# Attention scores in 64x32 tiles: 32 matmuls and one masked copy a pass, where 16 matmuls and three copies stood

## The chip, the core and the metric

The kernel runs on one core of a Trainium2 chip. A core has engines that work side by side, each through its own queue of instructions: PE (TensorE, matmuls, and PEld, its weight loads), DVE (VectorE), ACT (ScalarE), POOL (GpSimd) and SP, which here only issues DMAs. Matmul results land in PSUM; DVE and ACT bring them to SBUF. The metric is the device time of one execution in microseconds, as the median of the runs; less is better.

## What is computed

One layer in fp32 on x of shape (4, 2048, 256): a gated linear attention with a decaying state, a residual and a layer norm, then a feed-forward part with three coupling cycles, another residual and layer norm. The change touches the attention alone. Cut to that:

```python
Q = (xn @ WQ.T + bQ).reshape(batch, seq_len, N_HEADS, D_HEAD)   # 16 heads of 64
K = (xn @ WK.T + bK).reshape(batch, seq_len, N_HEADS, D_HEAD)
V = (xn @ WV.T + bV).reshape(batch, seq_len, N_HEADS, D_HEAD)
gate = silu(xn @ Wg.T + bg)
alpha = sigmoid(alpha_logit)
def step(h, qkv):
    q, k, v = qkv
    h = alpha[None, :, :, None] * h + k[:, :, :, None] * v[:, :, None, :]
    o = jnp.einsum('bhi,bhij->bhj', q, h)
    return (h, o)
...
y = (o * gate).reshape(batch, seq_len, D_INNER) @ WO.T + bO
```

The kernel does not step through the tokens. It cuts them into chunks of 64. Within a chunk, the output of a query at place t is the sum over keys at places s <= t of a decayed score times the value; what came before the chunk enters through the state. The decay between a key and a query is a product of a factor on the key and one on the query, each kept near 1 by measuring it from the middle of a block of 32 tokens.

## The kernel before

**Tiling.** A group is 512 tokens (G), eight chunks of 64 (C), each of two blocks of 32 (H). There are 4 x 4 groups, and in each the heads go in eight pairs (HP): 128 passes of the main loop in `fast_program` (L1060), which runs when the decay rates are mild (a flag computed at the start; a second program, for other rates, is not run here). A pass has 128 partitions: two heads of 64.

**What a pass does.** `inter` (L955, matmuls at L963) applies the state to the queries, in 64*64 tiles, into the PSUM tile `pu`. `all_scores` (L552) makes the scores of the pass in the PSUM tile `sc` through `pairs` (L541, matmuls at L547). `keys` (L600) transposes the next pass's keys with four matmuls (L604); `copy_first` (L557) and `copy_own` (L565) bring the scores to the SBUF tile `A`; `decayed` (L607, the multiplication is at L609) makes the next pass's decayed keys `KE` on DVE between the two. `values` (L192) projects a part of the values. `between` (L914) puts in steps of the output projection (L653) and the feed-forward part (L754 to L877) by an allowance of time kept in the code. `products` (L973, matmuls at L980) multiplies scores and values on top of `pu`; `updates` (L614, L620) makes the next pass's state updates in `sc`; `gated` (L985) takes `pu` out; `new_states` (L996, L630) steps the states; `projections` (L464, matmuls at L454) makes keys, queries and gate for the pass after next, on PE, with ACT taking them out (L468, L472, L484) and POOL scaling the queries (L500, L510, L514).

**Order.** The engines PE, DVE, ACT and POOL run in the order in which this code calls them (`manual_schedule`); waits between engines are put in by semaphores. `sc` has one buffer, shared by the scores and the updates; `A` has two, used in turn, filled with zeros once at the start.

**The scores.** For each of the four pairs of chunks (i) there are four matmuls, one for each head h and each chunk c of the pair. The stationary operand is the 64 features by 64 keys of the chunk; the moving one is 64 features by 96 columns, the tile `QF`: the chunk's 64 queries, each scaled from the middle of its own block, and then its 32 second-half queries once more, scaled for the keys of the first block (written at L510 and L514). The result is 64 keys by 96 columns: columns 0 to 63 are right for keys and queries of one block, columns 64 to 95 for first-block keys by second-block queries. The rest is not used.

**The copies.** `copy_first` takes columns 64 to 95 of the first block's keys to columns 32 to 63 of `A`, with one ACT copy for each chunk of a pair (32 partitions each, L563). `copy_own` then copies columns 0 to 63 over `A` on DVE where a mask says so (L568). The mask `masks["in"]` (L422 to L427) is 1 where the query is not before the key and both lie in one block, and elsewhere `A` keeps what it has: ACT's copy, or zero.

Of the kernel before, what the change touches and what calls it, by code (L numbers as in the profile page):

```python
# [37 lines left out]
F32 = mybir.dt.float32  # L41
# [3 lines left out]
ALU = mybir.AluOpType  # L45
AX = mybir.AxisListType

P = 128
# [6 lines left out]
C = 64  # L55
H = C // 2
# [3 lines left out]
NT = G // P  # L60
HT = 2 * NT
# [12 lines left out]
def post_norm_layer(ctx: ExitStack, tc: tile.TileContext, a: dict, out: bass.AP):  # L74
    nc = tc.nc
    x = a["x"]
# [148 lines left out]
    with ExitStack() as first:  # L225
        work = first.enter_context(tc.tile_pool(name="first", bufs=1))
# [87 lines left out]
    def layer(fast, inside):  # L314
        pool = inside.enter_context(tc.tile_pool(name="fixed", bufs=1))
        work = inside.enter_context(tc.tile_pool(name="work", bufs=1))
# [3 lines left out]
        def fixed(name, shape, dtype=F32):  # L320
            return pool.tile(shape, dtype, tag=name, name=name)
# [7 lines left out]
        def two_banks(tag, bufs):  # L329
            return psum.tile([P, 2, 512], F32, tag=tag, name=tag, bufs=bufs)  # L330
# [9 lines left out]
        def load_x(b, g):  # L340
            X[b, g] = tokens_at(b, g)
            nc.sync.dma_start(out=X[b, g], in_=tokens(b, g))

        def norm_x(b, g):

            xn[b, g] = xns[(b * NG + g) % 2]
            for _ in norm_steps(work, pj, X[b, g], xn[b, g], 4):
                yield
            residual(X[b, g])
            yield  # L350
# [27 lines left out]
        masks, qtab, ktab = {}, {}, {}  # L378
        blocks = {}

        def block_of(w):
            if w not in blocks:
                tw = work.tile([P, C], F32, tag="cs", name="tw", bufs=2)
                sw = fixed(f"sw{w}", [P, 1])
                for o, v in ((tw, trow), (sw, scol)):
                    if w > 1:
                        sh = work.tile(list(v.shape), I32, tag="t", name="sh", bufs=3 if fast else 2)
                        nc.vector.tensor_scalar(sh, v, w.bit_length() - 1, None, ALU.logical_shift_right)
                        v = sh
                    nc.vector.tensor_copy(o, v)  # L390
                blocks[w] = tw, sw
            return blocks[w]

        def mask(key, w, back, r, lo):

            tw, sw = block_of(w)
            masks[key] = fixed(f"mask{key[0]}_{key[1]}", [P, C // r * (r - lo)], U8)
            nc.vector.tensor_scalar(
                masks[key].rearrange("p (n x) -> p n x", x=r - lo),
                tw.rearrange("p (n l) -> p n l", l=r)[:, :, lo:], float(back), sw,  # L400
                ALU.subtract, ALU.is_equal,
            )

        def repeated(name, v, n):

            w = v.shape[2]
            if n == 1:
                return v
            t = fixed(name, [P, HP, n * w])
            nc.vector.tensor_copy(  # L410
                t.rearrange("p h (n w) -> p h n w", w=w), v.unsqueeze(2).to_broadcast([P, HP, n, w])
            )
            return t
# [6 lines left out]
        if fast:  # L420

            t1, s1 = block_of(1)  # L422
            th, sh = block_of(H)
            after = work.tile([P, C], F32, tag="t", name="after", bufs=3)
            nc.vector.tensor_scalar(after, t1, s1, None, ALU.is_ge)
            masks["in"] = fixed("mask_in", [P, C], U8)
            nc.vector.scalar_tensor_tensor(masks["in"], th, sh, after, ALU.is_equal, ALU.mult)  # L427
        else:
            mask((0, 0), 1, 0, C, 0)
            mask((1, 0), 1, 1, 2, 1)  # L430
            for w, r in STAGES[:2]:
                for o in range(r - 1):
                    mask((w, o), w, o + 1, w * r, (o + 1) * w)
            for w, r in STAGES:
                ktab[w] = repeated(f"ktab{w}", down[:, :, C - w : C], r - 1)
                for o in range(r - 1):
                    qtab[w, o] = repeated(
                        f"qtab{w}_{o}", up[:, :, w * o : w * o + w], (r - 1 - o) * C // (w * r)
                    )
# [22 lines left out]
        KF, QF = {}, {}  # L462
# [78 lines left out]
        def pairs(ps, k, q, col):  # L541

            n = q.shape[2]
            for i in range(NT):
                for h, c in ((0, 0), (1, 1), (0, 1), (1, 0)):
                    r = slice(h * 64, (h + 1) * 64)
                    tc.keep_in_program_order(nc.tensor.matmul(  # L547
                        ps[c * 64 : (c + 1) * 64, h, i * P + col : i * P + col + n],
                        k[r, 2 * i + c, :], q[r, 2 * i + c, :], start=True, stop=True,
                    ))  # L550

        def all_scores(it):  # L552
            ps = two_banks("sc", 1)
            pairs(ps, KF.pop(it), QF.pop(it), 0)
            return ps

        def copy_first(ps, A):  # L557

            pv = ps.rearrange("p h (i x) -> p (h i) x", x=P)
            av = A.rearrange("p h i t -> p (h i) t")  # L560
            for c in range(2):
                r = slice(c * C, c * C + H)
                nc.scalar.copy(av[r, :, H:], pv[r, :, C : C + H])  # L563

        def copy_own(ps, A):  # L565
            pv = ps.rearrange("p h (i x) -> p (h i) x", x=P)
            av = A.rearrange("p h i t -> p (h i) t")
            nc.vector.copy_predicated(av, masks["in"].unsqueeze(1).to_broadcast([P, HT, C]), pv[:, :, 0:C])  # L568

        def scores(it, n, A):  # L570

# [35 lines left out]
        def decayed(pt, it):  # L607
            ke = work.tile([P, NT, P], F32, tag="KE", name="KE", bufs=1)
            nc.vector.tensor_mul(  # L609
                ke, pt.rearrange("p (i x) -> p i x", i=NT), at(dtok, it[2], [P, NT, P])  # L610
            )
            return ke
# [290 lines left out]
        def add(queue, steps):  # L903
            queue.append([steps, next(steps)])
# [103 lines left out]
        def follow(n, k):  # L1008
            return its[n + k] if n + k < len(its) else None
# [50 lines left out]
        def fast_program():  # L1060


            groups = [(b, g) for b in range(B) for g in range(NG)]
            norms = {}

            def norm(k):
                if k < len(groups):
                    norms.setdefault(k, norm_x(*groups[k]))
                    next(norms[k])

            load_x(*groups[2])
            projections(its[0])
            KE[its[0]] = decayed(keys(its[0]), its[0])
            projections(its[1])
            ahead = new_states(its[0], updates(KE.pop(its[0]), its[0]))
            for n, it in enumerate(its):
                b, g, hp = it
                k = n // HP
                nxt, then = follow(n, 1), follow(n, 2)
                A = As[n % 2]  # L1080
                po = inter(it, *ahead)
                sc = all_scores(it)
                if nxt:
                    pt = keys(nxt)
                copy_first(sc, A)
                if nxt:
                    KE[nxt] = decayed(pt, nxt)
                copy_own(sc, A)
                if hp < 4:
                    values(b, g, 1, hp)  # L1090
                elif k + 1 < len(groups):
                    values(*groups[k + 1], 0, hp - 4)
                if hp == 7:
                    norm(k + 2)
                between(("pe", "dve", "act"), 1.4)
                products(it, po, A)
                if nxt:
                    us = updates(KE.pop(nxt), nxt)
                gated(it, po)
                if hp % 4 == 3:  # L1100
                    add(posts, post(b, g, hp // 4))
                if nxt:
                    ahead = new_states(nxt, us)
                if then:
                    projections(then)
                vector = 2.8
                if k == 0 and hp < 4:
                    vector = 0.0
                    if hp == 0:
                        residual(X0)  # L1110
                        ffn_constants()
                    norm(1)
                if hp == 4 and k and k + 2 < len(groups):
                    load_x(*groups[k + 2])
                if hp > 4:
                    norm(k + 2)
                    vector = 1.4
                between(("pe", "dve"), vector)

            while posts or nets or couples:  # L1120
                for queue, m in ((posts, 0), (nets, 0), (couples, 0), (couples, 1)):
                    if len(queue) > m and queue[m][1][2]():
                        run(queue, m)
# [45 lines left out]
```

## Time and profile before

| what | value |
|---|---|
| median of 3 runs | 1962.02 us (1960.25 to 1963.20) |
| profiled execution | 1961.66 us |
| its span in the profile | 1959.9 us |
| mean granted PE clock | 0.981 |
| instructions | 48150, of them 21070 matmuls and as many weight loads |
| DMA | 20 GB/s over the span |

The span runs from the first instruction to the last that the profiler saw; the rest of the execution lies around it. A group's row names line, engine, operation, what is written and read, the tile of the array for matmuls (rows*columns), shapes and count; after the bar come the busy time in us and the mean of one instruction in ns, after the next bar the engine's idle time before these instructions and what ended it. Ends of matmuls are modelled, so that one record is longer than the time until the next begins: a row's busy time is the union of its records. Some other groups of a pass, in the same form:

```profile
L500 POOL TENSOR_TENSOR qd<-QA,up 128x512 f32<-128x512 f32 x128 | 160.5, 1254 | 1169.9 <-ACT QA L472 1151.0
L468 ACT ACTIVATE KT<-pj,bK 128x512 f32<-128x512 f32 x128 | 87.9, 687 | 481.8 <-PE pj L454 481.8
L609 DVE TENSOR_TENSOR KE<-pj,dtok 128x512 f32<-128x512 f32 x128 | 88.1, 688 | 234.7 <-PE pj L604 234.4
L980 PE MATMUL pu<-A,V 64*64 64x64 f32 x4096 | 90.5, 227 | 39.2 <-DVE A L568 39.2
```

The chain that ended last is followed back from the last instruction to what released it, or to the one before it on its engine; it tells which work set the end.

### The profile page before, as it was taken

What the parts mean: (1) busy time and instruction counts of PE and PEld (TensorE: products, weight loads), DVE (VectorE), ACT (ScalarE), POOL (GpSimd) and SP (SyncE); (2) the same over time, 40 slices, a digit from 0 to 9 for tenths busy, and PEclk for the clock granted to TensorE, in tenths of its full rate; (3) what the DMA queues carried; (4) which work ended last, traced back from release to release, by engine and by line L of the source; (5) the groups of instructions that cost most, each with busy time, mean ns of one, the idle gap of its engine ahead of it and who ended that gap; (6) DMA issues with size and microseconds to landing.
All of it is one profiled execution on the core that took longest, in us unless ns stands there. A gap on an engine that the chain in (4) does not pass through costs nothing.

```text
span 1959.9 us, 48150 instructions
## 1 busy us (share of the span) xinstructions
PE 1860.1 (95%) x21070; PEld 1074.5 (55%) x21070; DVE 1216.3 (62%) x3054; ACT 812.4 (41%) x1299; POOL 452.7 (23%) x436
## 2 busy tenths in 40 slices
PE   7999999998999999999999999999999999999975
PEld 3565655655555555555555555555555555555531
DVE  4665656665775567755576656764558755666455
ACT  3223242222454445444345445544345544444344
POOL 1222222222222222222222222222212222122100
PEclk9999999999999999999999999999999999999986
DMA  4000000000011000100001000000000100000002
GB/s 155 2 2 23 2 23 2 23 2 23 2 34 33 2 23 2 45 23 2 23 2 45 23 2 23 21 30 17 12 13 12 39 18 12 2 23 34 1 11 67
DMA packets 27419, 41.67 MB, mean 21 GB/s; under 512 B 4032, under 2 KB 22336, under 8 KB 27200
## 3 DMA queue, kind: packets, MB, share of 16 engines
q1 hardware_dynamic: 26192, 38.48, 5.8%
q8 instruction: 168, 2.75, 0.6%
q14 instruction: 51, 0.42, 0.1%
q10 hardware_dynamic: 1008, 0.02, 0.0%
HBM read 21.72 MB, written 16.78 MB: 20 GB/s over the span
## 4 chain that ended last, share of the span: by engine, by line
PE 83%; DVE 11%; ACT 2%; issue 2%; POOL 1%; DMA 0%; DVEq 0%; ACTq 0%; POOLq 0%; SPq 0%
PE pj L454 31%; PE pj L653 11%; PE pj L192 9%; PE pj L754 6%; PE pu L963 4%; PE pu L980 4%; PE pj L798 4%; PE sc L547 4%; PE pj L604 3%; PE sc L620 3%; PE pj L804 1%; DVE t L781 1%; DVE u L785 1%; PE pj L813 1%; DVE states L630 1%
## 5 line engine op out<-in xcount | busy, mean ns | idle before, releaser
L500 POOL TENSOR_TENSOR qd<-QA,up 128x512 f32<-128x512 f32 x128 | 160.5, 1254 | 1169.9 <-ACT QA L472 1151.0
L468 ACT ACTIVATE KT<-pj,bK 128x512 f32<-128x512 f32 x128 | 87.9, 687 | 481.8 <-PE pj L454 481.8
L454 PE MATMUL pj<-xn,wK 128*128 128x512 f32 x512 | 258.1, 627 | 1.7 <-DVE sw L390 1.7
L454 PE MATMUL pj<-xn,wQ 128*128 128x512 f32 x512 | 240.6, 592 | 0.0
L454 PE MATMUL pj<-xn,wg 128*128 128x512 f32 x512 | 240.6, 592 | 0.0
L192 PE MATMUL pj<-wV,xn 128*128 128x512 f32 x496 | 235.2, 597 | 0.0
L609 DVE TENSOR_TENSOR KE<-pj,dtok 128x512 f32<-128x512 f32 x128 | 88.1, 688 | 234.7 <-PE pj L604 234.4
L630 DVE SCALAR_TENSOR_TENSOR states<-states,up,sc 128x64 f32<-128x64 f32 x768 | 215.8, 281 | 27.4
L653 PE MATMUL pj<-wO,og 128*128 128x256 f32 x1024 | 231.6, 379 | 0.0
L653 PEld LDWEIGHTS pj<-wO,og 128*128 128x128 f32 x1024 | 194.3, 190 | 52.7 <-issue 28.7
L658 DVE TENSOR_TENSOR X<-pj,X 128x512 f32<-128x512 f32 x64 | 44.2, 691 | 204.5 <-PE pj L653 204.5
L510 POOL TENSOR_TENSOR QF<-QA,qf 128x512 f32<-128x512 f32 x128 | 165.1, 1290 | 0.0
L454 PEld LDWEIGHTS pj<-xn,wQ 128*128 128x128 f32 x512 | 97.3, 190 | 122.5 <-issue 118.6
L454 PEld LDWEIGHTS pj<-xn,wg 128*128 128x128 f32 x512 | 97.3, 190 | 122.5 <-issue 114.8
L563 ACT COPY A<-sc 32x256 f32<-32x256 f32 x256 | 92.6, 362 | 156.7 <-PE sc L547 153.6
L472 ACT ACTIVATE QA<-pj,bQ 128x512 f32<-128x512 f32 x128 | 87.9, 687 | 140.4 <-PE pj L454 140.4
L980 PEld LDWEIGHTS pu<-A,V 64*64 64x64 f32 x4096 | 72.7, 136 | 118.8 <-DVE A L568 76.3
L454 PEld LDWEIGHTS pj<-xn,wK 128*128 128x128 f32 x512 | 88.7, 193 | 74.0 <-issue 65.3
L980 PE MATMUL pu<-A,V 64*64 64x64 f32 x4096 | 90.5, 227 | 39.2 <-DVE A L568 39.2
L192 PEld LDWEIGHTS pj<-wV,xn 128*128 128x128 f32 x496 | 85.5, 193 | 60.4 <-issue 60.4
L993 DVE TENSOR_TENSOR og<-pu,gate 64x256 f32<-64x256 f32 x256 | 108.1, 422 | 6.3
L484 ACT ACTIVATE gate<-pj,bg 128x512 f32<-128x512 f32 x128 | 88.0, 687 | 55.8 <-PE pj L454 41.7
(199 smaller groups left out, 2714.9 us busy)
## 6 DMA issues: line engine op xcount, KB each, us to landing
X<-in_x SPq DMA_DIRECT2D x16, 512.0 KB, 3.8
kept<-X SPq DMA_DIRECT2D x16, 512.0 KB, 2.6
out<-y SPq DMA_DIRECT2D x32, 256.0 KB, 2.1
x<-kept SPq DMA_DIRECT2D x14, 512.0 KB, 3.3
wV<-in_WV SPq DMA_DIRECT2D x1, 1024.0 KB, 6.7
wK<-in_WK SPq DMA_DIRECT2D x1, 1024.0 KB, 5.7
wQ<-in_WQ SPq DMA_DIRECT2D x1, 1024.0 KB, 7.9
wg<-in_Wg SPq DMA_DIRECT2D x1, 1024.0 KB, 7.5
```

Source lines behind the costliest of these rows:

```text
L192: nc.tensor.matmul(ps, xnT[:, k, i * P : (i + 1) * P], w_in["V"][:, k, half * 512 : (half + 1) * 512], start=(k == 0), stop=(k == KD - 1),)
L454: nc.tensor.matmul(ps, w_in[n][:, k, hp * P : (hp + 1) * P], xn[b, g][:, k, :], start=(k == 0), stop=(k == KD - 1),)
L484: nc.scalar.activation(gt, ps, AF.Silu, bias=b_in["g"][:, hp : hp + 1])
L500: nc.gpsimd.tensor_mul(qd, QA[it][:, :, 0:C], up[:, it[2], 1 : C + 1].unsqueeze(1).to_broadcast([P, NC, C]))
L510: nc.gpsimd.tensor_mul(qs[:, :, 0:C].rearrange("p c (n l) -> p c n l", l=H), qv.rearrange("p c (n l) -> p c n l", l=H), qf[:, hp, :].unsqu ...
L563: nc.scalar.copy(av[r, :, H:], pv[r, :, C : C + H])
L609: nc.vector.tensor_mul(ke, pt.rearrange("p (i x) -> p i x", i=NT), at(dtok, it[2], [P, NT, P]))
L630: nc.vector.scalar_tensor_tensor(o, before, up[:, hp, C : C + 1], u, ALU.mult, ALU.add)
L653: nc.tensor.matmul(ps[:, ii * D : (ii + 1) * D], og[b, g, hp][:, i * P : (i + 1) * P], wO[:, hp, :], start=(hp == hps[0]), stop=(hp == hps ...
L754: nc.tensor.matmul(ps, w[:, k, o * P : (o + 1) * P], x1[:, k, :], start=(k == 0), stop=(k == KD - 1))
L980: tc.keep_in_program_order(nc.tensor.matmul(po[place(h, c), c, i * C : (i + 1) * C], V[r, i, m + h, :], A[r, h, i, :], start=False, stop=T ...
L993: nc.vector.tensor_mul(ov[r, 1], pv[place(h, 1), 1], gv[r, 1])
```

## The change

The scores of a chunk and head are made by two matmuls instead of one, each for a block of 32 keys by all 64 queries of the chunk. Block 0's keys take the queries' first 32 columns and the third 32 (`qv[:, 0::2]`), block 1's keys the first and second (`qv[:, 0:2]`). The results lie at the 32 partitions of the block and at columns 0 to 63, where the products need them. The array is addressed in tiles of 64 rows by 32 columns, and in each i the eight matmuls name eight different places. The two ACT copies go. The masked DVE copy stays, after `decayed` as before; its mask is now "query not before key" alone, so the block numbers and the intermediate mask are no longer computed. In the built program the order of the other instructions on each engine is as before, except that one 128x64 fill with zeros (L417) moves from POOL to DVE. Lines after the first are moved by one to three.

```diff
         if fast:
             t1, s1 = block_of(1)
-            th, sh = block_of(H)
-            after = work.tile([P, C], F32, tag="t", name="after", bufs=3)
-            nc.vector.tensor_scalar(after, t1, s1, None, ALU.is_ge)
             masks["in"] = fixed("mask_in", [P, C], U8)
-            nc.vector.scalar_tensor_tensor(masks["in"], th, sh, after, ALU.is_equal, ALU.mult)
+            nc.vector.tensor_scalar(masks["in"], t1, s1, None, ALU.is_ge)
...
         def all_scores(it):
             ps = two_banks("sc", 1)
-            pairs(ps, KF.pop(it), QF.pop(it), 0)
+            k, q = KF.pop(it), QF.pop(it)
+            for i in range(NT):
+                for block in range(2):
+                    for h, c in ((0, 0), (1, 1), (0, 1), (1, 0)):
+                        r = slice(h * 64, (h + 1) * 64)
+                        at0 = c * C + block * H
+                        qv = q[r, 2 * i + c, :].rearrange("p (n l) -> p n l", l=H)
+                        tc.keep_in_program_order(nc.tensor.matmul(
+                            ps[at0 : at0 + H, h, i * P : i * P + C].rearrange("p (n l) -> p n l", l=H),
+                            k[r, 2 * i + c, block * H : (block + 1) * H],
+                            qv[:, 0:2] if block else qv[:, 0::2], start=True, stop=True,
+                        ))
             return ps
...
-        def copy_first(ps, A):
-            pv = ps.rearrange("p h (i x) -> p (h i) x", x=P)
-            av = A.rearrange("p h i t -> p (h i) t")
-            for c in range(2):
-                r = slice(c * C, c * C + H)
-                nc.scalar.copy(av[r, :, H:], pv[r, :, C : C + H])
-
-        def copy_own(ps, A):
-            pv = ps.rearrange("p h (i x) -> p (h i) x", x=P)
-            av = A.rearrange("p h i t -> p (h i) t")
-            nc.vector.copy_predicated(av, masks["in"].unsqueeze(1).to_broadcast([P, HT, C]), pv[:, :, 0:C])
+        def copy_scores(ps, A):
+            nc.vector.copy_predicated(
+                A.rearrange("p h i t -> p (h i) t"), masks["in"].unsqueeze(1).to_broadcast([P, HT, C]),
+                ps.rearrange("p h (i x) -> p (h i) x", x=P)[:, :, 0:C],
+            )
...
                 sc = all_scores(it)
                 if nxt:
                     pt = keys(nxt)
-                copy_first(sc, A)
                 if nxt:
                     KE[nxt] = decayed(pt, nxt)
-                copy_own(sc, A)
+                copy_scores(sc, A)
```

## The prediction

> **What bounds the kernel now.** I read the page first (busy shares, then the chain that ended last), then the groups by form, the waits, the chain of one heads pair, and the timeline there. A faster or slower run is told from no change beyond about 0.2%, 3.9 us here.
>
> ```profile
> PE 1860.1 (95%) x21070; PEld 1074.5 (55%) x21070; DVE 1216.3 (62%) x3054; ACT 812.4 (41%) x1299; POOL 452.7 (23%) x436
> PE 83%; DVE 11%; ACT 2%; issue 2%; POOL 1%; DMA 0%; DVEq 0%; ACTq 0%; POOLq 0%; SPq 0%
> ```
>
> PE sets the end: 83% of the chain is its own work, ACT has 2%. So an ACT instruction that goes is worth something only where PE waits for it, and PE time that comes or goes counts almost everywhere.
>
> ```profile
> L563 ACT COPY A<-sc 32x256 f32<-32x256 f32 x256 | 92.6, 362 | 156.7 <-PE sc L547 153.6
> L568 DVE COPY_PREDICATED A<-mask_in,sc 128x512 f32<-128x512 uint8 x128 | 92.0, 718 | 3.4 <-ACT A L563 2.7
> L547 PE MATMUL sc<-QF,KF 64*64 64x96 f32 x4096 | 109.6, 245 | 1.1
> ```
>
> The first two are the three copies of the description: two on ACT, one on DVE. The third is the scores: 16 matmuls for each of 128 passes (one heads pair of one 512-token group) show as 4096: each of these fp32 matmuls leaves two records, each with a weight load of its own.
>
> ```profile
> PE pu L980 <- DVE A L568: 39.2, 24, 3.9
> DVE A L568 <- ACT A L563: 2.7, 1, 2.7
> PE pj L798 <- ACT h L792: 10.7, 5, 5.9
> ```
>
> These are waits: who for whom, us in all, times, longest. PE's products (L980) wait for the finished scores in 24 passes of 128, and then it is DVE's queue that is late: the masked copy itself waited for ACT's copies once, 2.7 us.
>
> The chain through one pass, and a piece of it from the start of the kernel (start, us, what):
>
> ```profile
> 32.81 0.44 PE pj L604 x4
> ...
> 1044.05 0.62 PE pu L963 x32
> 1044.67 0.66 PE sc L547 x32
> 1045.34 0.59 PE pj L604 x4
> 1045.92 1.72 PE pj L192 x4
> ...
> 1052.81 0.62 PE pu L980 x32
> 1053.44 0.47 PE sc L620 x32
> ```
>
> L980 and L620 are the same shape (64*64 tiles, 64 moving columns, 32 records). L620 follows the same tiling and takes 0.47, or 0.058 for a round of four tiles; L980 follows matmuls of the whole array and takes 0.62. So **a change of tiling costs 0.15 us**. L604 says the same: at 32.81, after other matmuls of the whole array, its four take 0.44, and here, after the 64*64 tiles of L547, 0.59. L547 follows L963 in the same tiling and pays nothing on entering: 0.66 / 8 rounds = 0.0825 for 96 columns.
>
> ```profile
> 1043.98 0.14 PEld L963 LDWEIGHTS pu<-qd,carry 64*64 64x64 f32 x2 [0.33 <-issue]
> 1043.99 0.14 PEld L963 LDWEIGHTS pu<-qd,states 64*64 64x64 f32 x2
> 1044.03 0.14 PEld L963 LDWEIGHTS pu<-qd,carry 64*64 64x64 f32 x2
> 1044.49 0.84 PE L547 MATMUL sc<-QF,KF 64*64 64x96 f32 x32
> ```
>
> [...] L547's record spans 0.84 from first start to last end: less seven rounds of 0.0825 and one record of 0.245, 0.02 is left for the stagger of four tiles, 0.007 a tile.
>
> **The change, part by part.**
>
> *Scores on PE.* 16 matmuls of 64 keys by 96 columns become 32 of 32 keys by 64, so 64 records. In each of four steps the code names eight different places of the array (two row halves, four column strips) before it returns to the first. Each place then holds four matmuls, eight records. If the eight run side by side as the four do now, a pass has eight rounds of eight:
> - entering a new tiling (64*64 to 64*32): 0.15, of which 0.05 was the open load of 64 columns; 32 columns should take half, so 0.125. Bounds 0.12 to 0.15. Nothing shows this exact pair of tilings.
> - eight rounds of 64 columns: by L620's 0.058, 0.47; by L547's rate (0.0825 x 64/96 = 0.055), 0.44. L620's round is about its weight load (0.05 and a little), which halves, so I take the lower: 0.45.
> - four more tiles of stagger: 4 x 0.007 = 0.03.
> - leaving for L604's whole-array tiling: paid today too, 0.
>
> Sum 0.605 against 0.66: 0.055 less a pass. With the dear ends 0.65 (0.01 less), with the cheap ends 0.59 (0.07 less). In the 24 passes where PE waits for DVE anyway a shorter PE stretch gives nothing, so 104 x 0.055 = 5.7 us; the ends 1.0 and 7.3.
>
> *The two ACT copies go.* 256 x 362 ns = 92.6 us of ACT. I put 0 on the path: ACT stands idle 481.8 us before the key copies (KT, L468), so it catches up in every pass, and no L563 lies on the chain. What stood behind them in ACT's queue, the Gelu and its table load (L792), is released earlier; PE waits for that Gelu 10.7 us in all (5 times). Bounds 0 to 10.7 gained. A loss is excluded: nothing is added to ACT.
>
> *The masked copy* keeps its 128x512 and its 718 ns, and its place behind KE (L609) in DVE's queue. It now waits for PE instead of ACT. KE itself waits for L604, which stands behind the scores on PE, so when KE ends the scores are long done: 0. That cover, KE's 688 ns, also hid the ACT pair. Its single wait of 2.7 us may go: 0 to 2.7, in the same bound.
>
> *The mask* is built with five small DVE operations fewer, and a small fill moves from POOL to DVE. In the timeline the old ones run from 27.3 to 28.5 us, while DVE next waits until 30.13 for KT. 0, bounds 0 and 0.3 (one of its 0.28 operations) either way.
>
> *Records on PE:* 4096 matmuls and as many loads more. The fastest sustained run in the trace is 32 pairs in 0.47, 14.7 ns a pair, and there the tiles set it; the starts of four tiles 0.007 apart show at least bursts of 7 ns a pair. The new scores need 64 pairs in 0.48, 7.5 ns a pair. (To fetch them costs no time that shows: the instruction queue q8 moved 2.75 MB in 0.6% of the span, and gets about a sixth more.) This is the weak point, and the first two rivals hang on it.
>
> Sum: 5.7 us less. The profiled execution took 1961.66 (span 1959.9 and 1.8 around it), which becomes 1956.0; the median of the runs is 0.4 above it, so **1956.4 us**, 0.29% less.
>
> [...]
>
> **The rivals.**
>
> 1. *Slower: four tiles at a time, not eight.* The column strips of one row half would share what today feeds two tiles. Then a pass has 16 rounds: 0.125 + 16 x 0.057 + 0.02 = 1.06, 0.40 more, x 104 = 41 us: 1962.0 + 41 = 2003. For it: the trace has no tile of 32 columns, and never more than two tiles at work in one row half. [...] It decides as soon as a round of eight takes more than (0.66 - 0.125 - 0.03) / 8 = 0.063; at that point the change is worth nothing.
>
> 2. *Slower: instructions don't arrive fast enough.* Eight tiles run, but pairs come every 10 ns once the queue is drained, say: 64 x 10 = 0.64, with 0.125 0.765; 0.105 x 104 = 11 us, 1973. Between the 8.4 ns that cost nothing (0.535 / 64) and the sustained 14.7 (1.07, as in 1) everything is open, 1962 to 2003. For it: nothing faster than 14.7 lasts longer than a burst. Against it: the weight loads of L547 stood idle for want of issue 2.4 us in the whole span.
>
> 3. *A larger gain.* Going from 64*64 to 64*32 empties nothing, since the row halves stay: 0.125 falls off too, 0.18 x 104 = 19 us; or ACT's release pays its 10.7. 1943 to 1951. Against it: the chain shows 0.15 for every other change of shape.
>
> **How the numbers follow.** Forecast 0.53, own range 1954 to 1961; rival 1 0.19, rival 2 0.19, rival 3 0.09. I give the forecast the most since the independence of the tiles is a row of the timeline, and the eight places are a fact of the code; the two slower ones get 0.38 together because nothing in the trace runs eight tiles. Three quarters of the forecast lie below 1958.1 (the 0.2% bound), a quarter within; of rival 2 a quarter within, the rest above. Faster 0.53 x 0.75 + 0.09 = 0.49; same 0.53 x 0.25 + 0.19 x 0.25 = 0.18; slower 0.19 + 0.19 x 0.75 = 0.33. The range runs from 1945, inside rival 3, to 1992, most of rival 2; it leaves out rival 1 and the far ends, some 2 in 10.
>
> **What would show it.** In the changed profile: the scores as 8192 matmuls of 64*32, their chain piece near 0.60 (rival 1: 1.06; rival 2: 0.7 to 1.0 with uneven starts in the second half); idle time of about 0.1 before their first weight load, which rival 3 lacks; L604's piece unchanged at 0.59; no A<-sc on ACT, whose busy time falls by 93; the masked copy waiting for PE hardly ever, and the waits of L980 for it near 24. The forecast is wrong if the eight tiles don't run abreast, and too small if PE's waits for ACT fall by more than a few us.

## The result and the profile after

The change makes the kernel slower: 1973.76 us in the median of four runs (1972.72 to 1976.15) against 1961.13 in four of the kernel before beside them, a ratio of 1.0068 with an interval from 1.0050 to 1.0085. The profiled execution took 1972.72 us (span 1970.9), 11.1 more than the profiled one of before. The forecast of 1956.4 had the wrong sign; the time lies inside the range, where rival 2 put it.

The page of the changed kernel, its parts on busy time, on the DMA queues, on the chain and on groups:

```profile
PE 1871.0 (95%) x25166; PEld 1084.4 (55%) x25166; DVE 1217.5 (62%) x3050; ACT 721.5 (37%) x1043; POOL 453.1 (23%) x435
...
q8 instruction: 200, 3.28, 0.7%
...
PE 83%; DVE 11%; ACT 2%; issue 2%; POOL 1%; DMA 0%; DVEq 0%; ACTq 0%; POOLq 0%; SPq 0%
...
L560 PE MATMUL sc<-QF,KF 64*32 64x64 f32 x8192 | 115.5, 227 | 1.1
```

The change does what it says: 8192 records of 64*32 in place of 4096 of 64*64, and 90.9 us of ACT's work gone. PE sets the end as before (83% of the chain). The scores' row grew from 109.6 to 115.5 us although each matmul streams a third fewer columns; there are twice as many of them, and eight places to run in instead of four.

The group of the masked copy, and PE's waits (in all, times, longest):

```profile
L568 DVE COPY_PREDICATED A<-mask_in,sc 128x512 f32<-128x512 uint8 x128 | 91.8, 717 | 2.1 <-PE sc L560 2.1
```

```profile
PE pu L983 <- DVE A L568: 38.0, 24, 3.7
PE pj L801 <- ACT h L795: 11.3, 5, 6.5
```

No wait moved: the products wait for DVE 24 times as before (39.2 us then), PE waits 11.3 us for the Gelu where it was 10.7, and the masked copy hardly ever waits for the scores. The loss is PE's own time. The chain through a pass (start, us, what; x counts the records that lie on the chain, here 53 of 64) shows where:

```profile
1023.65 0.62 PE pu L966 x32
1024.27 0.81 PE sc L560 x53
1025.09 0.59 PE pj L607 x4
1025.67 1.72 PE pj L193 x4
```

The state's matmuls, the key transposes and the values have the lengths of before. The scores' piece alone went from 0.66 to 0.81. Its inside is read from the starts of the scores' matmul records, in ns from the first one of the pass, as the median over the passes:

```
record              1    8    9   16   17   24   25   32   33   34   40   48   56   64
before, L547        0  105  168  270  333  435  498  600
changed, L560       0   47   80  127  136  183  192  238  267  323  409  490  567  668
```

The first 32 records run much as the forecast had it: eight starts 6.7 ns apart, the second round 80 ns behind the first and each later one 56 ns behind the one before it, four rounds in 238 ns. Then the pattern breaks, in every one of the 128 passes: after the 33rd weight load the next one comes 55 to 107 ns later, 77 in the median, and the one behind it 56 in the median. From the 35th load to the 64th it is 288 ns, 9.9 a pair.

The whole section, by medians: from the state's last record to the first score 38 ns before and 148 now; first to last score 600 and 668; last score to the first key transpose 173 and 147. Together 0.811 and 0.963 us: 0.152 more, x 104 = 15.8. The main loop (from the first record of the products to the last) took 1804.9 us before and takes 1820.3: 15.4 more. That is 4.4 us more than the span grew; the rest comes back behind the loop. The stretch behind the last products, of the kernel before and of the changed one (stretch, length, busy time of PE, PEld, DVE, ACT and POOL, granted clock, DMA):

```profile
1849.70:1959.90 110.20, 75.36 (x232) 33.83 (x221) 56.88 (x153) 45.29 (x83) 4.28 (x3) 0.79 0.10 35
```

```profile
1865.30:1970.90 105.60, 69.33 (x232) 31.30 (x223) 56.88 (x153) 45.24 (x83) 4.28 (x3) 0.86 0.11 36
```

The work is the same (232 matmuls, DVE's 56.88 us to the digit), but the granted clock is 0.79 in one and 0.86 in the other: 47.3 us of the old tail lie in stretches of half clock, and 30.5 of the new one. So 15.4 in the loop, 0.2 ahead of it and -4.5 behind make the 11.1. The 4.5 are thus not put down to less work; they go with where the half-clock stretches fall.

### The profile page after: what moved, and what is told of

Same layout as the page of the kernel before. It is cut to its first block, busy times and chain, and to the rows that moved or that the text cites. A ratio compares the mean times of both kernels' runs of the same rounds, so it can differ in the third digit from the quotient of the medians.

```text
span 1970.9 us, 56079 instructions
## 1 busy us (share of the span) xinstructions
PE 1871.0 (95%) x25166; PEld 1084.4 (55%) x25166; DVE 1217.5 (62%) x3050; ACT 721.5 (37%) x1043; POOL 453.1 (23%) x435
## 4 chain that ended last, share of the span: by engine, by line
PE 83%; DVE 11%; ACT 2%; issue 2%; POOL 1%; DMA 0%; DVEq 0%; ACTq 0%; POOLq 0%; SPq 0%
PE pj L452 30%; PE pj L656 11%; PE pj L193 9%; PE pj L757 6%; PE sc L560 4%; PE pu L966 4%; PE pj L801 4%; PE pu L983 4%; PE pj L607 3%; PE sc L623 3%; PE pj L807 1%; DVE t L784 1%; DVE u L788 1%; DVE states L633 1%; PE pj L816 1%
## 5 line engine op out<-in xcount | busy, mean ns | idle before, releaser
L560 PE MATMUL sc<-QF,KF 64*32 64x64 f32 x8192 | 115.5, 227 | 1.1
L966 PE MATMUL pu<-qd,states 64*64 64x64 f32 x3584 | 109.7, 225 | 0.2 <-DVE states L631 0.2
```

Source lines behind the costliest of these rows:

```text
L560: tc.keep_in_program_order(nc.tensor.matmul(ps[at0 : at0 + H, h, i * P : i * P + C].rearrange("p (n l) -> p n l", l=H), k[r, 2 * i + c, bl ...
L966: tc.keep_in_program_order(nc.tensor.matmul(po[place(h, c), c % 2, c // 2 * C : (c // 2 + 1) * C], state[r, :], qd[r, c, :], start=(c < 2) ...
```

## The experiments

All times are medians; each ratio is to runs of the kernel before on the same chip.

| label | us | ratio | interval |
|---|---|---|---|
| before_no_act_copies | 1960.95 | 0.9997 | 0.9988 to 1.0006 |
| before_one_switch | 1978.66 | 1.0087 | 1.0072 to 1.0103 |
| after_reversed | 1976.17 | 1.0075 | 1.0056 to 1.0093 |
| after_short_streams | 1967.65 | 1.0034 | 1.0021 to 1.0047 |
| after_again (the changed kernel) | 1971.99 | 1.0051 | 1.0034 to 1.0068 |
| after_split_by_state | 1988.60 | 1.0134 | 1.0118 to 1.0151 |
| after_split_by_keys | 1984.22 | 1.0109 | 1.0092 to 1.0125 |
| after_long_streams_between | 2012.48 | 1.0267 | 1.0232 to 1.0301 |
| after_scores_twice | 2062.83 | 1.0523 | 1.0488 to 1.0559 |
| after_stop_between | 2180.93 | 1.1129 | 1.1096 to 1.1161 |

**What the ACT copies were worth.** The kernel before without them (the scores of first-block keys by second-block queries are then missing):

```diff
-                copy_first(sc, A)
```

> The kernel before without its two ACT copies of a pass (left out: the scores of first-block keys by second-block queries, which then stay zero); PE's work is unchanged. Theory (ACT's copies lie on no path that sets the end): within 0.2% of the kernel before, so 1958 to 1965 us, and PE's wait for the Gelu stays near 11 us. Rival (the release of ACT pays back part of the loss that the change made elsewhere): 5 to 11 us faster, 1950 to 1956.

Measured: no change (0.9997). Its wait for the Gelu, which stands behind those copies in ACT's queue:

```profile
PE pj L798 <- ACT h L792: 10.7, 5, 5.9
```

The same 10.7 us as with the copies. ACT's 92.6 us lay beside other work throughout: this part of what the change removes is worth nothing.

**What a change of tiling costs.** The kernel before with the last of its four steps in 64x32 tiles (8 matmuls of 32 keys in place of 4 of 64), 96 columns as before: 40 records a pass, and one more change of tiling:

```diff
+                for b0, w in ((0, C),) if i < NT - 1 else ((0, H), (H, H)):
...
+                            ps[c * C + b0 : c * C + b0 + w, h, i * P : i * P + n],
+                            k[r, 2 * i + c, b0 : b0 + w], q[r, 2 * i + c, :], start=True, stop=True,
```

> [...] Theory: each pass 0.08 to 0.12 us longer by the change of tiling alone, 8 to 15 us slower than before. Rival (a change from 64*64 to 64*32 empties nothing, and the whole loss is the feed): within 3 us of before.

Measured: 17.4 us more, above what was expected. The chain of one pass:

```profile
1052.10 0.62 PE pu L972 x32
1052.73 0.82 PE sc L560 x40
1053.55 0.59 PE pj L613 x4
```

The step from the last 64*64 record to the first 64*32 one is 173 ns (from 435 to 608 by the medians), and 62 ns from round to round without a change: 0.11 us for the change of tiling, the same as the 148 - 38 of the changed kernel. The 16 records behind it run eight abreast and show no break. The section grew by 0.161 in all. The other 0.05 is what the expectation left out: eight tiles start over 47 ns instead of 20, and the second round comes 106 ns behind the first where it was 82. The last score to the first key transpose is 173 ns as before.

**Does the break belong to certain matmuls?** The order of the four steps turned round:

```diff
-            for i in range(NT):
+            for i in reversed(range(NT)):
```

> The changed kernel with the four steps of the scores in the opposite order (i = 3, 2, 1, 0). Theory (PE's queue of instructions is full when the scores begin and runs empty after 32 pairs; what follows is paced by the feed): the first 32 records again in rounds of 8 at 0.056 us, a gap after the 32nd, then some 9 us per 1000 pairs, 0.67 us from first to last start, and the time of the changed kernel within 3 us. Rival (the matmuls of the later steps are slow for what they read or write, addresses or PSUM columns): the slow records come first, the fast ones last.

Measured: every median of the starts shown above is the same to the nanosecond. The break belongs to the number in the row, not to a matmul or its place in PSUM.

**Is the slow part paced by the streams?** Half the columns in each matmul (first-block keys by second-block queries are left out):

```diff
-                            ps[at0 : at0 + H, h, i * P : i * P + C].rearrange("p (n l) -> p n l", l=H),
+                            ps[at0 : at0 + H, h, i * P : i * P + H],
...
-                            qv[:, 0:2] if block else qv[:, 0::2], start=True, stop=True,
+                            qv[:, block], start=True, stop=True,
```

> The changed kernel with 32 moving columns in each score matmul instead of 64 (left out: first-block keys by second-block queries), with the same 64 records a pass, the same tiling and a masked copy of the same size. Theory (the feed paces the second half): 0.60 to 0.67 us from first to last start instead of 0.67, and 0 to 6 us off the changed kernel's time. Rival (the array or its reads pace it, so that half the columns take half the time): 0.35 us from first to last start, 30 us or more off.

Measured: 6.1 us less than the changed kernel's 1973.76 (4.3 less than its 1971.99 in the table). First to last start is 0.590 us, just under the expected range and far from the rival's 0.35. The first 32 records now start within 169 ns instead of 238, and the break is at the same number. The starts of the weight loads, in ns from the first one, as medians:

```
load                    1   32   33   34   35   40   48   56   64
changed, 64 columns     0  186  195  273  328  379  457  538  616
32 columns              0  134  145  247  278  329  407  487  566
```

Half the streaming takes 29% off the first part, but from the 35th load to the 64th both take 288 ns. So the second part is not paced by the streams.

**Is it how many come in a row?** Two ways of breaking the 64 pairs into 32 and 32. In both, `half_scores` makes two of the four steps, and `all_scores` now only the first two. First, half of the scores in front of the state's matmuls, half behind:

```diff
-                po = inter(it, *ahead)
-                sc = all_scores(it)
+                sc, kf_it, qf_it = all_scores(it)
+                po = inter(it, *ahead)
+                half_scores(sc, kf_it, qf_it, 1)
```

> The changed kernel with its scores in two halves: steps 0 and 1 (32 records) before the state's matmuls (inter, 32 records in 64*64 tiles), steps 2 and 3 after them. One more change of tiling a pass (0.09 and an open load), and time for PE's queue to fill again. Theory (the records after the 32nd are slow only because the queue has run empty): both halves 0.24 us from first to last start, no gap after the 32nd; two halves of 0.29 against 0.72 save 0.14 and the extra change costs 0.12, so 0 to 4 us faster than the changed kernel, 1969 to 1975. Rival (the second half is slow in itself, whatever stands before it): its starts spread over 0.4 us as now, 14 to 18 us slower, 1987 to 1993.

The chain of one pass, and two of PE's waits:

```profile
1059.72 0.39 PE sc L563 x32
1060.10 0.62 PE pu L968 x32
1060.73 0.38 PE sc L563 x32
1061.11 0.59 PE pj L609 x4
```

```profile
PE sc L563 <- DVE carry L635: 30.2, 14, 3.0
...
PE sc L563 <- DVE states L635: 7.4, 4, 1.9
```

Both halves take 0.238 us from first start to last, with no break, and each pays the change of tiling. In a pass without waits the section is 0.046 us shorter than the changed kernel's, in spite of one change of tiling more: so far the theory. But the kernel is 16.6 us slower than the changed one. The scores now stand first, and `sc` is not free until DVE has read the last state update out of it: 37.6 us of waits, 18 times, that weren't there. The state's matmuls used to work through that same time, one as each state came; their row fell from 109.7 to 89.6 us. On top, stretches of half clock grew from 27.3 to 47.8 us in the loop. Of the 17.3 us by which the profiled span is longer than the changed kernel's, 10.3 lie in the loop, 4.6 in the tail (from 105.5 to 110.1 us) and 2.4 ahead of the loop. How the loop's share divides between waits and clock was not measured.

Second, half of the scores behind the key transposes:

```diff
-                sc = all_scores(it)
+                sc, kf_it, qf_it = all_scores(it)
                 if nxt:
                     pt = keys(nxt)
+                half_scores(sc, kf_it, qf_it, 1)
```

> The changed kernel with steps 2 and 3 of its scores behind the key transposes (four 128x128 matmuls, 0.44 us, 8 records). Two more changes of tiling a pass (into 64*32: 0.09 and a load of 0.03; out of it: 0.09 and an open load of 0.11). Theory (queue): both halves 0.24 us from first to last start; 0.31 for the changes less 0.14 saved, 0.17 more a pass, 18 to 23 us slower than the changed kernel, 1991 to 1998. Rival (slow in itself): 0.31 more a pass, 33 to 40 us slower.

```profile
1035.72 0.39 PE sc L563 x32
1036.10 0.59 PE pj L609 x4
1036.69 0.38 PE sc L563 x32
1037.08 1.91 PE pj L193 x4
```

Again 0.238 us in both halves. From the last transpose to the first score are 0.202 us, and from the last score to the values 0.146, where 0.109 lay between transposes and values: 0.239 more for one tiling put between. The values behind it take 1.91 instead of 1.72, 0.10 of it between their own records. With 0.19 less for the halves a pass comes out 0.15 us dearer, 15.6 in all; the products wait 3.8 us less for DVE, which leaves 11.8. The median is 12.2 more than the changed kernel's 1971.99, but the agreement is partly luck: the four executions took 1981.0, 1981.3, 1987.2 and 1987.3 us, and the profiled one, from which the sum is read, is 15.4 above the profiled changed kernel beside it (1971.83), 14.2 of it in the loop. Either way it is below the expected 18 to 23. That the rival's 33 to 40 fails does not hang on this. The changes of tiling cost a little more than the 0.31 expected (0.34 with the 0.10 in the values); the halves saved more (0.19 instead of 0.14), and the shorter waits were not foreseen.

**Does the pace last?** All 64 records made twice:

```diff
-            for i in range(NT):
+            for i in [*range(NT), *range(NT)]:
```

> The changed kernel with all 64 records of the scores made twice, one set behind the other. Theory (behind the first 32 pairs the instructions' arrival sets the pace, and goes on to): 64 more pairs at 9.5 ns, 0.61 us a pass, first to last start 1.28 us in place of 0.67; x 104 = 63 us, 2032 to 2038. Rival (one pause in a section, and no lasting pace): the second set runs eight abreast, 0.44 us a pass, x 104 = 46 us, 2015 to 2021. If fast stretches of 32 come back after each pause, the starts show it.

```profile
1067.08 0.62 PE pu L966 x32
1067.71 1.55 PE sc L560 x91
```

```profile
PE sc L560 <- issue: 14.4, 13, 1.8
```

The pace lasts: from the 48th to the 120th load 10.4 ns a pair, without another fast stretch; first to last 1.37 us. The rival falls. The time, 2062.8, is above the 2032 to 2038 expected: the pace is 10.4 and not 9.5, and 14.4 us of a new kind came in, 13 stalls of up to 1.8 us in the scores in which PE waits for nothing that the profile shows. Missing instructions would fit, but no view tells. The section grew by 0.70 us in the median, x 104 = 73; with the stalls that makes the 87 us by which the loop grew. Among PE's waits in the changed kernel there is no such one in the scores.

**What brings the fast starts back?** Eight more matmuls of 192 columns in the same tiles between the halves:

```diff
+                for block in range(2 if i == 2 else 0):
...
+                        tc.keep_in_program_order(nc.tensor.matmul(
+                            ps[at0 : at0 + H, h, 256:448],
+                            k[r, 2 * i + c, block * H : (block + 1) * H],
+                            q[r, 4:6, :], start=True, stop=True,
+                        ))
```

> The changed kernel with eight more matmuls (16 records) in the same 64x32 tiles between the two halves of the scores, each streaming 192 columns; their results are overwritten by the second half. Theory (a stock of some 32 pairs of instructions is used up by the first half, and is filled again while PE streams for long): 192 columns last about 0.16 us a record by the 0.0825 of 96, so two rounds take 0.33 us, in which at 9.5 ns a pair some 35 pairs arrive; the second half's 32 records then run eight abreast again, first to last start about 0.24 us. A pass costs 0.33 - 0.20 = 0.13 us more than the changed kernel, x 104 = 14 us: 1984 to 1988. Rival (the second half is slow for a reason of its own, such as its places in PSUM or its number in the pass): its records keep 9.5 ns a pair, 0.29 to 0.43 us, and a pass costs 0.33 more, x 104 = 34 us: 2004 to 2008.

```profile
1016.16 0.38 PE sc L569 x32
1016.54 0.41 PE sc L559 x10
1016.95 0.39 PE sc L569 x27
```

Both forecasts fell: the second half takes 0.469 us from first start to last (its last 30 records 0.382), not 0.24 and not the rival's 0.29 to 0.43, and the time, 2012.5, is above even the rival's. Eight abreast did not come back behind the long streams. The starts suggest why: the long matmuls themselves come one in 17 ns within each eight, right behind the break, and the loads go on through the streams, so that nothing would pile up behind them. That is a reading that no view shows, and the next run was made to decide between it and the rival.

**A stop without a change of tiling.** One column of the keys is made to depend, at no change in value, on a result of the first half:

```diff
+                if i == 2:
+                    one = k[:, 4, 0:1]
+                    nc.vector.scalar_tensor_tensor(one, ps[:, 0, 0:1], 0.0, one, ALU.mult, ALU.add)
```

> The changed kernel with a short stop of PE between the two halves of the scores and no change of tiling: a DVE operation on 128x1 elements reads one column of the first half's result and adds nought times it to one column of the keys that the second half reads. [...] Theory (the stock of 32 pairs fills whenever PE stands still, at 8.4 to 9.5 ns a pair some 0.3 us for all of it): the second half's 32 records run eight abreast as the first, first to last start about 0.24 us, without the step of 0.08 behind the 32nd. Rival (only a change of tiling fills it): its starts come every 8.4 to 9.5 ns a pair, 0.27 us or more, uneven, 17 ns from one matmul to the next. The time only tells how long the stop is: 0.1 to 0.3 us a pass more than the changed kernel, 1982 to 2003, and more where DVE is behind.

The chain of one pass:

```profile
1060.48 0.52 PE sc L563 x32
1061.00 0.02 issue
1061.02 0.17 DVE KF L557
1061.19 0.04 issue
1061.24 0.46 PE sc L563 x32
```

In the 71 passes in which the stop was shortest (0.56 to 0.68 us from the last start of one half to the first of the other) the second half takes 0.243 us in the median, eight abreast, with no break. No pass of the 128 shows the slow pattern; where the half takes longer, up to 0.373 us, it is at half clock, wholly or in part. So a stop of PE between the halves brings the fast pattern back with no change of tiling, as the two splits did with one; the rival falls. The 0.1 to 0.3 us a pass put on the stop was the author's estimate, and no run shows it: in the pass above DVE's part of the chain is 0.23 us with the two short pieces of issue around it, and the stops come to 197 us over the passes, 1.5 each. So the time, far above what was expected, only says that DVE is late; and many stops are followed by half clock (below).

## Why the prediction was wrong

*The bound* was right: PE's own time decides, and no other engine's wait moved by more than 1.2 us.

*Entering the new tiling*, put at 0.125 (0.12 to 0.15): measured 0.110 up to the first score, in two kernels, a little below the bounds. No run shows an open load by itself. What the profiles show is a longer first round: the second round of scores starts 80 ns behind the first where later ones are 56 apart, 0.024 more, which makes 0.134. On entering 64x64 tiles (the state's matmuls, L963, in the profile of before) it is 107 ns against 58, 0.049, near the forecast's 0.05. That 32 columns take half of 64 was an estimate; with four 64x64 tiles a load starts 55 ns or more behind the fourth load before it, with eight 64x32 tiles 28 or more behind the eighth.

*Stagger*, put at 0.03: eight starts take 47 ns where four took 20, 0.027.

*Leaving for the whole array*, put at 0: 147 ns instead of 173, a small gain that was left out.

*Eight rounds of 64 columns at 0.45*: this is the step that failed. Its rate was right, 0.056 a round within the first four once the first round (0.080) is over, and at that rate the whole section would have been 0.148 + 0.462 + 0.147 = 0.757, which is 0.054 below before, the forecast's own 0.055. But the rate held for four rounds and not for eight: first to last start is 0.668 instead of 0.462. These 0.21 us, from the fifth round on, turn -0.05 into +0.15.

The step rested on "the new scores need 64 pairs in 0.48, 7.5 ns a pair", and was called the weak point there. Two arguments were set against rival 2, and neither could carry it. Four starts 7 ns apart are a burst of four; they do not say how long a row can come at that pace. And that the old scores hardly stood idle for issue says only that 0.600 / 32, 18.8 ns a pair, is slow enough. A burst was read as a rate.

*Rival 2* is what happened in its main point: pairs come at about 10 ns behind the first 32, and uneven starts in the second half were named as its mark. Its shape was different: 32 pairs for nothing, a pause (77 and 56 ns between loads), then 10 to 11 ns a pair, rather than a pace from the first pair on. That its 1973 was hit is partly luck: it had 11 us of loss for the scores, the loop lost 15.4, and the 4.5 that the tail gave back were in no forecast. *Rival 1* falls: eight tiles do run abreast (eight starts in 47 ns, the next round 80 behind the first, then 56). *Rival 3* falls in both parts, since the tiling change costs 0.11 and ACT's release nothing.

*ACT at 0, the masked copy at 0, the mask at 0* were right: ratio 0.9997 without the copies; the masked copy's wait 2.1 us; the first products 0.2 us later than before. *The 104 passes* were right: 15.4 / 0.152 = 101. In the profiles the sections of the 103 passes in which the products do not wait grew by 15.4 us together, which is the growth of the loop.

*The tail* was in no term of the sum. It moved by -4.5 us with the half-clock stretches, more than the 3.9 us that were named as the least that can be told from no change.

No run with all the scores is faster than the kernel before. The 64x32 tiles keep their pace for 32 pairs only, and even cut into two halves, with no break, a pass costs 2.408 us from the start of the last PE record before the section to the first of the values, against 2.454 in the changed kernel and 2.304 before the change (medians). Fewer instructions for the same scores might help; that was not tried.

What stays open: where the pace of 10 to 11 ns a pair is set, in fetching the instructions, in decoding them or elsewhere on their way, which no view tells apart, and what the pause behind the 33rd load is made of. Every run whose inside is read here carries the profiler's records, so a part of theirs in the pace is not ruled out. What the experiments do show is that the slow part hangs on how many pairs come without a break, not on which matmuls they are or on whether they stream 64 columns or 32.

## What to carry to other kernels

When a change cuts matmuls into more and smaller ones, set the instructions a section needs in a row against two rates, not one: what comes at once after a break (here 32 pairs) and what arrives behind it (here 10.4 ns a pair, sustained). A fast start of a few records in the trace shows only the first of the two; look for the longest run at that pace before it goes into a sum. And give each new tiling between two others its price (0.11 us here from 64x64 to 64x32, about 0.24 for the way into it and out again between whole-array matmuls) before counting what the smaller tiles save.

## What the runs showed of the hardware

*32 pairs at once behind a break.* Behind each break seen with 32 pairs or more after it (a change of tiling, or a stop of 0.56 us and more at full clock) 32 matmuls start in four rounds of eight: eight starts 6.7 ns apart, 0.238 us from the first to the last in the changed kernel, 0.243 behind the stop, 0.169 with half the columns. In the changed kernel the load behind the 33rd then comes 77 ns later and the one behind it 56, and from there it is one pair in 10 to 11 ns (9.9 from the 35th to the 64th load, the same with half the columns; 10.4 from the 48th to the 120th in the longer row). What holds the 32 pairs no view shows: a stock that is used up and filled again is the author's reading of these starts.

*Tiles beside each other.* In the profile of before the first loads of four 64x64 tiles (L547, L620, L963, L980) start within 20 ns by the medians. No load there starts less than 55 ns behind the fourth load before it, and no matmul less than 58 behind the fourth matmul before it with 64 moving columns, 82 with 96. In the changed kernel the first eight matmuls in 64x32 tiles start within 47 ns, and the 9th to the 32nd each 55 ns or more behind the eighth before it.

*Half clock behind long waits.* In the run with the stop, 208.2 us of the loop went at half clock, against 27.3 in the changed kernel, and the mean granted clock fell from 0.985 to 0.944. The second half of the scores ran at half clock, wholly or in part (0.33 to 0.37 us instead of 0.243), in 24 of the 27 passes with a stop of over 3.0 us, in 5 of the 30 between 0.7 and 3.0, and in 2 of the 71 below 0.7, one of which was at half clock before the stop. So in this run a long wait mostly cost more than itself.
